# Three partial products of one tile: two PSUM banks joined on VectorE, or one bank scaled in place by ScalarE

## The chip, the cores and the metric

The kernel runs on one core of one Trainium2 chip. The metric is the device time of that core in microseconds, from the first instruction to the last. The five engines of the core are written PE (TensorE: matmuls; PEld are its weight loads), DVE (VectorE), ACT (ScalarE), POOL (GpSimd) and SP (the queue that starts most transfers).

## The reference, cut to what matters

The input is 64 batches of 256 rows by 512 columns. Two layers follow one another, each of the form "add to x, then normalise each row".

```python
q = x @ Wq + bq;  k = x @ Wk + bk;  v = x @ Wv + bv        # 8 heads of 64
scores = q @ k^T / 8, masked by adj                         # per batch and head, 256 x 256
attn = softmax(scores);  out = (attn @ v) @ Wo + bo
x = layernorm(x + out)                                      # layer 0
y = adj @ x                                                 # per batch
x = layernorm(x + y @ weight + bias)                        # layer 1
```

All arrays are float32. The change concerns only the three products q, k and v.

## The kernel before, in words

**Pairs and windows.** The 64 batches are worked in 32 pairs, two batches at a time, so that a product with 128 columns of weights and a pair's 512 rows is one PSUM tile of 128 x 512 float32 (a bank). The program is unrolled: one "window" for each pair. A window holds the four attention units of its own pair (`scores` at L391, the exponentials at L395, `values` at L418 and L426), and between them the products q, k, v of the next pair and the rest of the pair before: the projection with Wo (`o_proj`), the product with adj (`adj_x`, L541) and layer 1's product (`last`).

**Who decides the order.** TensorE's order is written out by hand: the function `between(w)` returns the list of steps of one window, in which an entry `None` (a "slot") stands for the `values` of one unit and the `scores` of the next. The other engines' orders come from a scheduler that puts instructions by its own estimate of when they are ready. Each engine then works through its list in that order. Small steps that VectorE does later are put off by a count of steps (`later`, `tick`).

**The products q, k, v.** In this profile a 128x512 matmul on whole float32 operands (L343) lasts 592 to 649 ns in the mean, and one on parts of the type fp32r (L350) 389 to 423 ns. From the third pair on each operand is therefore split in parts: x into `high`, `low` and `diff` (`XG`, `XL`, `XD` in the code; `x_parts`, L176 to L178, and `x_high`, L321), and each weight likewise, once, into three parts that lie in DRAM and are streamed back in a ring of five buffers named `wr` (`load_w`, L141, issued by GpSimd). A tile of q, k or v is the sum of three products of parts; `FINE` is 4096:

```python
tile = (1 + 1/FINE) * (high @ w_high + low @ w_low) + diff @ w_diff
```

Each product is a group of four matmuls (L350). `part_products` puts the first two into one bank, called near, and the third into another, called far. `joined` brings them together: ScalarE evicts near to SBUF with the scale (and the bias of q or k) at L355, and VectorE adds far to that at L357. There are 12 such tiles in a window (four each of v, q and k); q and k tiles go to `qT` and `kT`, v tiles to `v`. The first two pairs have no parts: there each tile is one product on the whole float32 operands (L343).

**Other products.** `o_proj` and `last` use a scheme of seven block products instead of eight (`SEVEN`, `block_product`, L281), each of eight matmuls, whose results VectorE adds to the rows `r` (L331, L502). The sums of blocks that they need are made by VectorE at L241. After the last block VectorE takes the statistics (L467, L468), adds epsilon (`ve`, L473), GpSimd takes the power -1/2 (`rstd`, L475), and the rows are normalised: in layer 0 by VectorE (L489), in layer 1 by ScalarE (L487, after `less` at L477). For `adj_x` the normalised rows are split once more, `hl` and `ys`, the high part by ScalarE (L526), the low one by VectorE (L527).

**Attention.** Exponentials from PSUM by ScalarE (L395), mask by VectorE (L400), sum of the two key halves (L406); the row sums and the weighted values are evicted by ScalarE to `zc` (L420) and `vc` (L429); VectorE turns the sums around (`z`, L436; reciprocal, L439; `zc`, L441) and divides (`o`, L442). The biases are added to the rows at L458. The next pair's x is transposed by VectorE (L311).

**PSUM.** There are two pools of four banks each: `ps_at` (tiles named `at`) for attention, `ps_mm` (tiles named `mm`) for all else.

Of a middle window, `between` gave this order before (v, q, k are whole tiles; o, y, l are `o_proj`, `adj_x`, `last`):

```python
seq = slot + v[:2] + o[:1] + v[2:3] + o[1:2] + v[3:] + o[2:3] + slot + o[3:4] + q[:1] + o[4:5] + q[1:2] + \
    o[5:] + q[2:] + slot + y[:2] + k[:1] + y[2:] + k[1:2] + bo_steps[:1] + l[:1] + k[2:3] + bo_steps[1:] + \
    l[1:2] + k[3:] + after_k
```

It is followed by a slot and the other five blocks of `last`, mixed with the transposes and splits of the pair after next.

Of the kernel before, what the change touches and what calls it, by code (L numbers as in the profile page):

```python
# [20 lines left out]
F32 = mybir.dt.float32  # L21
F32R = mybir.dt.float32r
I32 = mybir.dt.int32
AF = mybir.ActivationFunctionType
OP = mybir.AluOpType
AX = mybir.AxisListType

P = 128
# [3 lines left out]
FINE = 4096.0  # L32
# [5 lines left out]
def tile_adj_resnorm(tc, x, adj, wq, bq, wk, bk, wv, bv, wo, bo, w1, b1, out):  # L38
    good = fast(tc, x, adj, wq, bq, wk, bk, wv, bv, wo, bo, w1, b1, out)
    with tc.If(good < P):  # L40
        general(tc, x, adj, wq, bq, wk, bk, wv, bv, wo, bo, w1, b1, out)


def fast(tc, x, adj, wq, bq, wk, bk, wv, bv, wo, bo, w1, b1, out):

    nc = tc.nc
    B, N, D = x.shape
    HD = D // H
    DC = D // P
    NC = N // P  # L50
    NP = B // 2
# [21 lines left out]
    four = pool("four", 4)  # L73
    small = pool("small", 2)
    ps_at = pool("ps_at", 4, space=bass.MemoryType.PSUM)
    ps_mm = pool("ps_mm", 4, space=bass.MemoryType.PSUM)

    XC, R, XF, XG, XL, XD, Q, K, V, E, SM, O, HL, Y, ST = ({} for _ in range(15))
# [23 lines left out]
    def weights(name, w, b12, queue, by_head=False):  # L102

        t = W[name] = cpool.tile([P, 7, 2, HF], F32, name="w" + name)
        b12 = B12[name] = one.tile([P, 2, 2, HF], F32, name=b12)[:, 0]
        for to, k, n in ((t[:, 0], 0, 0), (t[:, 1], 1, 0), (b12, 0, 1), (t[:, 2], 1, 1)):
            quarter = w[k * HF:(k + 1) * HF, n * HF:(n + 1) * HF]
            if by_head:  # L110
                for a in range(2):
                    queue.dma_start(to[:, a], quarter.rearrange("(h a i) e -> a h i e", h=4, a=2)[a])
            else:
                queue.dma_start(to, quarter.rearrange("(c p) e -> p c e", p=P))
# [9 lines left out]
    def by_partition(b, name):  # L124
        t = cpool.tile([P, DC], F32, name=name)
        nc.sync.dma_start(t, b.rearrange("(c p) -> p c", p=P))
        return t
# [7 lines left out]
    WP, SCRATCH = {}, {}  # L135
# [8 lines left out]
    FIRST = {}  # L144
# [40 lines left out]
    bq_s, bk_s = by_partition(bq, "bq"), by_partition(bk, "bk")  # L185
# [83 lines left out]
    BANKS = {}  # L269
# [63 lines left out]

    def part_products(name, p, j, rows_first):


        near = ps_mm.tile([P, D], F32, name="mm")
        if p < 2:  # L340
            for k in range(DC):
                left, right = (XF[p, k], FIRST[name, k]) if rows_first else (FIRST[name, k], XF[p, k])
                nc.tensor.matmul(near, left[:, j * P:(j + 1) * P], right, start=k == 0, stop=k == DC - 1)  # L343
            return near, None
        far = ps_mm.tile([P, D], F32, name="mm")
        for i, (xs, to) in enumerate(((XG, near), (XL, near), (XD, far))):
            for k in range(DC):
                a, b = xs[p, k], WP[name, p, i](k)
                left, right = (a, b) if rows_first else (b, a)
                nc.tensor.matmul(to, left[:, j * P:(j + 1) * P], right, start=k == 0 and i != 1,  # L350
                                 stop=k == DC - 1 and i != 0)
        return near, far

    def joined(to, near, far, **kw):
        nc.scalar.activation(to, near, AF.Identity, scale=1 + 1 / FINE if far else 1.0, **kw)  # L355
        if far:
            nc.vector.tensor_tensor(to, to, far, op=OP.add)  # L357

    def q_or_k(p, j, is_k):
        T, b, name = (K, bk_s, "k") if is_k else (Q, bq_s, "q")  # L360
        g, a = divmod(j, 2)
        if a == 0:
            T[p, g] = qk.tile([P, 2, 2, N], F32, name=name + "T")
        joined(T[p, g][:, a].rearrange("p b i -> p (b i)"), *part_products(name, p, j, False), bias=b[:, j:j + 1])

    def v_rows(p, j):
        b, c = divmod(j, 2)
        if c == 0:
            V[p, b] = four.tile([P, NC, D], F32, name="v")
        joined(V[p, b][:, c], *part_products("v", p, j, True))  # L370

    def q_cols(p, j):
        q_or_k(p, j, False)

    def k_cols(p, j):
        q_or_k(p, j, True)

# [244 lines left out]
    def between(w):  # L624

        pre = [w + 1] if w + 1 < NP else []
        post = [w - 1] if w >= 1 else []
        a = lambda f, n: [(f, p, i) for p in pre for i in range(n)]
        z = lambda f, n: [(f, p, i) for p in post for i in range(n)]
        o, l, y = z(o_proj, 7), z(last, 7), z(adj_x, 4)  # L630
        v, q, k = a(v_rows, 4), a(q_cols, 4), a(k_cols, 4)
        bo_steps = [(with_bo, w, b) for b in range(2) if 0 <= w < NP]
        x_steps = [(x_t, w + 2, i) for i in range(4) if w + 2 < NP]
        x_parts_ = [(x_parts, w + 2, i) for i in range(4) if w + 2 < NP]
        x_all = [s for pair in zip(x_steps, x_parts_) for s in pair]
        load = lambda *what: [(load_w, n, w + 1 + d, i) for n, d, i in what]
        slot = [None]
        if w == -1:
            seq = [(x_t, 0, i) for i in range(4)]
            split_v, split_q = ([(split_w, n, i) for i in range(4)] for n in "vq")  # L640
            for i in range(4):
                seq += v[i:i + 1] + split_v[i:i + 1]
            for i in range(4):
                seq += q[i:i + 1] + split_q[i:i + 1]
            seq += [(adj_t,)]
            for i in range(4):
                seq += k[i:i + 1] + x_steps[i:i + 1]
            return seq + load(("v", 2, 0), ("v", 2, 1), ("v", 2, 2), ("q", 2, 0), ("q", 2, 1))
        if w == 0:
            weights("1", w1, "hl", nc.sync)  # L650
            split_k = [(split_w, "k", i) for i in range(4)]
            return slot + v + [(weight_sums, "1"), (weights, "o", wo, "hl", nc.sync, True)] + slot + q[:3] + split_k + \
                slot + q[3:] + k[:1] + [(bv_wo,), (weight_sums, "o"), (load_r, 0)] + k[1:2] + slot + k[2:] + bo_steps + \
                x_all + [(load_r, 1)]
        v += load(("q", 0, 2), ("k", 0, 0), ("k", 0, 1))
        q += load(("k", 0, 2), ("v", 1, 0), ("v", 1, 1))
        after_k = load(("v", 1, 2), ("q", 1, 0), ("q", 1, 1)) if w + 2 < NP else []
        seq = slot + v[:2] + o[:1] + v[2:3] + o[1:2] + v[3:] + o[2:3] + slot + o[3:4] + q[:1] + o[4:5] + q[1:2] + \
            o[5:] + q[2:] + slot + y[:2] + k[:1] + y[2:] + k[1:2] + bo_steps[:1] + l[:1] + k[2:3] + bo_steps[1:] + \
            l[1:2] + k[3:] + after_k  # L660
        if w < NP - 2:
            return seq + slot + [s for i in range(5) for s in l[2 + i:3 + i] + x_all[2 * i:2 * i + 2]]
        o0 = [(part, w, 0, 0, i) for i in range(7)]
        return seq + l[2:3] + slot + l[3:4] + o0[:1] + l[4:5] + o0[1:3] + l[5:6] + o0[3:5] + l[6:] + o0[5:]

    def window(w):
        units = [(w - 1, 3)] + [(w, u) for u in range(4)]
        for step in between(w):
            if step is None:
                before = units.pop(0)  # L670
                if before[0] >= 0:
                    values(*before)
                scores(*units[0])
            else:
                f, *args = step
                f(*args)
            tick()
# [195 lines left out]
```

## Time and profile before

| what | value |
| --- | --- |
| time, median of 3 runs | 2662.22 us (2661.95 to 2664.72) |
| span of the profiled run | 2662.8 us |
| PE busy | 2588.0 us, 97% |
| DVE busy | 2108.1 us, 79% |
| ACT busy | 962.5 us, 36% |
| POOL busy | 288.0 us, 11% |
| additions at L357, q, k and v, 120 each | 82.3, 82.2 and 82.1 us of DVE |
| evictions at L355, q, k and v, 128 each | 87.4, 88.2 and 72.8 us of ACT |

Busy times are sums over the span. Matmuls are pipelined, and the ends that the profile gives them are modelled, so a PE that is busy need not be at its peak; starts of matmuls are what one can measure distances with. Busy time of an engine says nothing about whether the end waits for that engine: for this one reads the chain of waits, which is followed back from the last instruction, at each step to what released it.

### The profile page before, as it was taken

Reading aid. Unit: us, or ns where it says so; the run is one execution under the profiler, and the core shown is the slowest. Engines: PE = TensorE matmul, PEld = TensorE weight load, DVE = VectorE, ACT = ScalarE, POOL = GpSimd, SP = SyncE. Lnnn points to the kernel's source line nnn. Section 1 sums busy time; section 2 is a strip of 40 time slices with the busy share of each in tenths; the row PEclk is TensorE's granted clock in tenths of the full one; section 3 lists DMA queues with packets and bytes.
Section 4 is the critical chain, followed back from the end, with each engine's and each line's share of the span. In section 5 each row is a group of like instructions: output and inputs, shape, how many; then the busy total and the mean of one; then the engine's idle time right before and its main releaser. Section 6 shows DMA issues by size and latency. Waiting matters only on the chain.

```text
span 2662.8 us, 41800 instructions
## 1 busy us (share of the span) xinstructions
PE 2588.0 (97%) x16326; PEld 1990.5 (75%) x16326; DVE 2108.1 (79%) x3561; ACT 962.5 (36%) x1710; POOL 288.0 (11%) x610
## 2 busy tenths in 40 slices
PE   9999999999999999999999999999999999999997
PEld 4577777777777777777777777777777777777775
DVE  3777878878788778788787888787887788887877
ACT  4433333333333333333333333333333333333333
POOL 0011101111101111011111011110111110111000
PEclk9999999999999999999999999999999999999999
DMA  9444655544564536554545555365545455454310
GB/s 274 133 150 136 184 149 150 151 164 153 144 189 134 164 132 188 143 162 140 174 143 154 179 143 159 137 180 143 173 139 169 138 165 168 143 159 149 121 37 29
DMA packets 346987, 402.04 MB, mean 151 GB/s; under 512 B 270240, under 2 KB 272544, under 8 KB 312224
## 3 DMA queue, kind: packets, MB, share of 16 engines
q0 software_dynamic: 38880, 283.13, 29.0%
q1 hardware_dynamic: 307360, 115.13, 20.3%
q8 instruction: 130, 2.13, 0.3%
q10 hardware_dynamic: 544, 1.05, 0.1%
q14 instruction: 73, 0.60, 0.1%
HBM read 356.26 MB, written 42.99 MB: 150 GB/s over the span
## 4 chain that ended last, share of the span: by engine, by line
PE 68%; DVE 21%; ACT 5%; issue 4%; POOL 1%; DMA 1%; DVEq 0%; SPq 0%; POOLq 0%; ACTq 0%
PE mm L350 30%; PE mm L281 19%; PE mm L541 5%; PE at L391 5%; PE at L426 4%; DVE e L400 3%; DVE xT L311 3%; DVE st L467 3%; ACT r L487 3%; PE mm L343 2%; DVE diff L178 2%; DVE low L177 2%; DVE sm L406 1%; DVE r L331 1%; PE at L418 1%
## 5 line engine op out<-in xcount | busy, mean ns | idle before, releaser
L400 DVE TENSOR_TENSOR e<-e,adjT 128x1024 f32<-128x1024 f32 x256 | 307.1, 1221 | 27.7 <-ACT e L395 27.7
L350 PE MATMUL mm<-high,wr 128*128 128x512 f32 x960 | 288.0, 421 | 0.0
L395 ACT ACTIVATE e<-at 128x512 f32<-128x512 f32 x512 | 269.4, 596 | 49.1 <-PE at L391 49.0
L391 PE MATMUL at<-qT,kT 64*128 64x256 f32 x2048 | 264.0, 393 | 7.7 <-ACT zc L420 4.0
L281 PE MATMUL mm<-wo,o 128*128 128x256 f32 x1024 | 249.1, 385 | 15.9 <-ACT v L355 15.9
L350 PE MATMUL mm<-low,wr 128*128 128x512 f32 x960 | 257.9, 390 | 0.0
L350 PE MATMUL mm<-diff,wr 128*128 128x512 f32 x960 | 256.7, 389 | 0.0
L391 PEld LDWEIGHTS at<-qT,kT 64*128 64x128 f32 x2048 | 197.0, 187 | 75.8 <-issue 53.0
L426 PE MATMUL at<-e,v 128*32 128x256 f32 x4096 | 244.5, 379 | 0.0
L281 PEld LDWEIGHTS mm<-wo,o 128*128 128x128 f32 x1024 | 189.2, 189 | 63.6 <-ACT v L355 28.1
L281 PE MATMUL mm<-w,o 128*128 128x256 f32 x992 | 235.9, 380 | 0.0
L331 DVE TENSOR_TENSOR r<-r,mm 128x512 f32<-128x512 f32 (+1 forms) x204 | 132.3, 650 | 120.9 <-PE mm L281 120.8
L355 ACT ACTIVATE qT<-mm,bq 128x512 f32<-128x512 f32 x128 | 87.4, 683 | 364.7 <-PE mm L350 353.6
L350 PEld LDWEIGHTS mm<-low,wr 128*128 128x128 f32 x960 | 180.3, 188 | 40.2
L281 PEld LDWEIGHTS mm<-w,o 128*128 128x128 f32 x992 | 186.0, 190 | 30.4 <-issue 0.3
L350 PEld LDWEIGHTS mm<-diff,wr 128*128 128x128 f32 x960 | 180.2, 188 | 37.9
L281 PE MATMUL mm<-w,ys 128*128 128x256 f32 x720 | 179.1, 392 | 26.3 <-DVE r L502 26.3
L350 PEld LDWEIGHTS mm<-high,wr 128*128 128x128 f32 x960 | 176.7, 188 | 30.1
L426 PEld LDWEIGHTS at<-e,v 128*32 128x32 f32 x4096 | 133.1, 110 | 87.9
L321 ACT ACTIVATE high<-x 128x512 fp32r<-128x512 f32 x120 | 75.7, 630 | 305.7 <-DVE x L176 235.3
L281 PEld LDWEIGHTS mm<-w,ys 128*128 128x128 f32 x720 | 129.6, 189 | 71.2 <-DVE r L502 37.9
L502 DVE TENSOR_TENSOR r<-r,mm 128x512 f32<-128x512 f32 x240 | 162.1, 675 | 21.9 <-PE mm L281 21.9
(141 smaller groups left out, 4106.9 us busy)
## 6 DMA issues: line engine op xcount, KB each, us to landing
wr<-v POOLq DMA_DIRECT2D x90, 1024.0 KB, 8.0
wr<-q POOLq DMA_DIRECT2D x90, 1024.0 KB, 7.9
wr<-k POOLq DMA_DIRECT2D x90, 1024.0 KB, 6.9
r<-in_x_dram SPq DMA_DIRECT2D x32, 1024.0 KB
x<-in_x_dram SPq DMA_DIRECT2D x496, 64.0 KB
out_dram<-r SPq DMA_DIRECT2D x60, 512.0 KB
out_dram<-r SPq DMA_DIRECT2D x8, 256.0 KB
o<-in_L_gnn_Wv_dram ACTq DMA_DIRECT2D x2, 512.0 KB
```

Of the source, the lines that this page charges most:

```text
L281: nc.tensor.matmul(pm[:, j, :], left[:, k, j * P:(j + 1) * P], right[:, k, :], start=begins and j == 0 and k == 0, stop=k == 1, skip_group ...
L311: nc.vector.transpose(XF[p, i], xs)
L331: nc.vector.tensor_tensor(to, to, pm, op=OP.add)
L350: nc.tensor.matmul(to, left[:, j * P:(j + 1) * P], right, start=k == 0 and i != 1, stop=k == DC - 1 and i != 0)
L355: nc.scalar.activation(to, near, AF.Identity, scale=1 + 1 / FINE if far else 1.0, **kw)
L391: nc.tensor.matmul(sc[s][:, a, :], K[p, g][r, a, b, kc * P:(kc + 1) * P], Q[p, g][r, a, b, :], start=True, stop=True)
L395: nc.scalar.activation(e[:, s], sc[s], AF.Exp, scale=qscale)
L400: nc.vector.tensor_tensor(e, e, mask[:, kc:kc + 1, :].to_broadcast([P, 4, N]), op=OP.mult)
L426: nc.tensor.matmul(at[h * 32:(h + 1) * 32, a, :], V[p, b][:, kc, col:col + 32], e[kc][:, h % 2, h // 2, :], start=kc == 0, stop=kc == NC - 1)
L467: nc.vector.bn_stats(st, R[p][:, b, c, :])
L502: assembled(i, pm, out, lambda to, pm, half: nc.vector.tensor_tensor(to, to, pm, op=OP.add))
L541: nc.tensor.matmul(pm[:, j, :], hl[:, i, mc, j * P:(j + 1) * P], adjT[:, mc, :], start=mc == 0 and i == 0, stop=mc == NC - 1 and i == 1)
```

## The change

All three products go into one bank. `near` makes the first two, and ScalarE then multiplies the bank in place by 1 + 1/4096 (PSUM to PSUM). `far` has TensorE add the third product to the scaled contents (its first matmul doesn't set the flag that begins a new sum), and ScalarE evicts the finished tile, with the bias for q and k. VectorE's addition of far is gone. A tile so needs one bank where it needed two, but its three products can't follow one another directly: the third waits for the scaling. The written order therefore puts other work between a tile's near and its far.

```diff
-    def part_products(name, p, j, rows_first):
...
-        far = ps_mm.tile([P, D], F32, name="mm")
-        for i, (xs, to) in enumerate(((XG, near), (XL, near), (XD, far))):
...
-    def joined(to, near, far, **kw):
-        nc.scalar.activation(to, near, AF.Identity, scale=1 + 1 / FINE if far else 1.0, **kw)
-        if far:
-            nc.vector.tensor_tensor(to, to, far, op=OP.add)
+    def near(name, p, j):
...
+        pm = BANKS[name, p, j] = ps_mm.tile([P, D], F32, name="mm")
...
+        for i, xs in enumerate((XG, XL)):
+            part_product(pm, name, p, j, i, xs)
+        nc.scalar.activation(pm, pm, AF.Copy, scale=1 + 1 / FINE)
+    def part_product(pm, name, p, j, i, xs):
+        for k in range(DC):
+            nc.tensor.matmul(pm, *operands(name, j, xs[p, k], WP[name, p, i](k)), start=i == 0 and k == 0,
+                             stop=k == DC - 1, skip_group_check=True)
+    def far(name, p, j):
+        pm = BANKS.pop((name, p, j))
+        if p > 1:
+            part_product(pm, name, p, j, 2, XD)
+        if name == "v":
...
+            nc.scalar.activation(V[p, b][:, c], pm, AF.Copy)
+            return
...
+        nc.scalar.activation(T[p, g][:, a].rearrange("p b i -> p (b i)"), pm, AF.Identity, bias=bias[:, j:j + 1])
```

The order of a middle window becomes this, with vn, qn, kn for the near and vf, qf, kf for the far steps. The loads of weight parts (not shown) are moved along with the steps that last read a buffer.

```diff
-        seq = slot + v[:2] + o[:1] + v[2:3] + o[1:2] + v[3:] + o[2:3] + slot + o[3:4] + q[:1] + o[4:5] + q[1:2] + \
-            o[5:] + q[2:] + slot + y[:2] + k[:1] + y[2:] + k[1:2] + bo_steps[:1] + l[:1] + k[2:3] + bo_steps[1:] + \
-            l[1:2] + k[3:] + after_k
+        seq = slot + vn[:2] + vf[:1] + o[:1] + vf[1:2] + vn[2:3] + o[1:2] + vf[2:3] + vn[3:] + o[2:3] + vf[3:] + slot + \
+            o[3:4] + qn[:1] + o[4:5] + qf[:1] + qn[1:2] + o[5:6] + qf[1:2] + qn[2:3] + o[6:] + qn[3:] + qf[2:3] + slot + \
+            qf[3:] + y[:2] + kn[:1] + y[2:] + kf[:1] + kn[1:2] + bo_steps[:1] + kn[2:3] + kf[1:2] + l[:1] + kf[2:3] + \
+            kn[3:] + bo_steps[1:] + l[1:2] + kf[3:]
```

In the text below, L numbers are those of the kernel before unless it says otherwise.

More of the change, by code (lines that the diff above doesn't have):

```diff
@@ L331, in assembled @@
             nc.vector.tensor_tensor(to, to, pm, op=OP.add)
-    def part_products(name, p, j, rows_first):
-        near = ps_mm.tile([P, D], F32, name="mm")
+    def near(name, p, j):
+        pm = BANKS[name, p, j] = ps_mm.tile([P, D], F32, name="mm")
         if p < 2:
[L341 to L344, printed above, removed]
-        far = ps_mm.tile([P, D], F32, name="mm")
-        for i, (xs, to) in enumerate(((XG, near), (XL, near), (XD, far))):
[L347 to L352, printed above, removed]
@@ L354, in joined @@
-    def joined(to, near, far, **kw):
-        nc.scalar.activation(to, near, AF.Identity, scale=1 + 1 / FINE if far else 1.0, **kw)
-        if far:
-            nc.vector.tensor_tensor(to, to, far, op=OP.add)
-    def q_or_k(p, j, is_k):
-        T, b, name = (K, bk_s, "k") if is_k else (Q, bq_s, "q")
+            whole_product(pm, name, p, j)
+            return
+        for i, xs in enumerate((XG, XL)):
+            part_product(pm, name, p, j, i, xs)
+        nc.scalar.activation(pm, pm, AF.Copy, scale=1 + 1 / FINE)
@@ new lines, in operands, with whole_product @@
+    def operands(name, j, rows, w):
+        left, right = (rows, w) if name == "v" else (w, rows)
+        return left[:, j * P:(j + 1) * P], right
+    def whole_product(pm, name, p, j):
+        for k in range(DC):
+            nc.tensor.matmul(pm, *operands(name, j, XF[p, k], FIRST[name, k]), start=k == 0, stop=k == DC - 1)
+    def part_product(pm, name, p, j, i, xs):
+        for k in range(DC):
+            nc.tensor.matmul(pm, *operands(name, j, xs[p, k], WP[name, p, i](k)), start=i == 0 and k == 0,
+                             stop=k == DC - 1, skip_group_check=True)
@@ L361, in q_or_k @@
+    def far(name, p, j):
[3 more added lines that the diff above has]
+        if name == "v":
+            b, c = divmod(j, 2)
+            if c == 0:
+                V[p, b] = four.tile([P, NC, D], F32, name="v")
+            nc.scalar.activation(V[p, b][:, c], pm, AF.Copy)
+            return
+        T, bias = (K, bk_s) if name == "k" else (Q, bq_s)
         g, a = divmod(j, 2)
@@ L363, in q_or_k @@
             T[p, g] = qk.tile([P, 2, 2, N], F32, name=name + "T")
[L364 to L376, printed above, removed]
+        nc.scalar.activation(T[p, g][:, a].rearrange("p b i -> p (b i)"), pm, AF.Identity, bias=bias[:, j:j + 1])
     UNITS = [(g, b) for g in range(2) for b in range(2)]
@@ L627, in between @@
         post = [w - 1] if w >= 1 else []
-        a = lambda f, n: [(f, p, i) for p in pre for i in range(n)]
         z = lambda f, n: [(f, p, i) for p in post for i in range(n)]
         o, l, y = z(o_proj, 7), z(last, 7), z(adj_x, 4)
-        v, q, k = a(v_rows, 4), a(q_cols, 4), a(k_cols, 4)
+        first, then = ([[(f, n, p, j) for j in range(4) for p in pre] for n in "vqk"] for f in (near, far))
         bo_steps = [(with_bo, w, b) for b in range(2) if 0 <= w < NP]
@@ L637, in between @@
         slot = [None]
+        if w < 1:
+            v, q, k = ([s for pair in zip(m, n) for s in pair] for m, n in zip(first, then))
         if w == -1:
@@ L641, in between @@
             for i in range(4):
-                seq += v[i:i + 1] + split_v[i:i + 1]
+                seq += v[2 * i:2 * i + 2] + split_v[i:i + 1]
             for i in range(4):
-                seq += q[i:i + 1] + split_q[i:i + 1]
+                seq += q[2 * i:2 * i + 2] + split_q[i:i + 1]
             seq += [(adj_t,)]
             for i in range(4):
-                seq += k[i:i + 1] + x_steps[i:i + 1]
+                seq += k[2 * i:2 * i + 2] + x_steps[i:i + 1]
             return seq + load(("v", 2, 0), ("v", 2, 1), ("v", 2, 2), ("q", 2, 0), ("q", 2, 1))
@@ L651, in between @@
             split_k = [(split_w, "k", i) for i in range(4)]
-            return slot + v + [(weight_sums, "1"), (weights, "o", wo, "hl", nc.sync, True)] + slot + q[:3] + split_k + \
-                slot + q[3:] + k[:1] + [(bv_wo,), (weight_sums, "o"), (load_r, 0)] + k[1:2] + slot + k[2:] + bo_steps + \
+            return slot + v + [(weight_sums, "1"), (weights, "o", wo, "hl", nc.sync, True)] + slot + q[:6] + split_k + \
+                slot + q[6:] + k[:2] + [(bv_wo,), (weight_sums, "o"), (load_r, 0)] + k[2:4] + slot + k[4:] + bo_steps + \
                 x_all + [(load_r, 1)]
-        v += load(("q", 0, 2), ("k", 0, 0), ("k", 0, 1))
-        q += load(("k", 0, 2), ("v", 1, 0), ("v", 1, 1))
-        after_k = load(("v", 1, 2), ("q", 1, 0), ("q", 1, 1)) if w + 2 < NP else []
-        seq = slot + v[:2] + o[:1] + v[2:3] + o[1:2] + v[3:] + o[2:3] + slot + o[3:4] + q[:1] + o[4:5] + q[1:2] + \
-            o[5:] + q[2:] + slot + y[:2] + k[:1] + y[2:] + k[1:2] + bo_steps[:1] + l[:1] + k[2:3] + bo_steps[1:] + \
-            l[1:2] + k[3:] + after_k
+        (vn, qn, kn), (vf, qf, kf) = first, then
+        vn += load(("q", 0, 2), ("k", 0, 0))
+        vf += load(("k", 0, 1))
+        qn += load(("k", 0, 2), ("v", 1, 0))
+        qf += load(("v", 1, 1))
+        kn += load(("v", 1, 2), ("q", 1, 0))
+        kf += load(("q", 1, 1))
+        seq = slot + vn[:2] + vf[:1] + o[:1] + vf[1:2] + vn[2:3] + o[1:2] + vf[2:3] + vn[3:] + o[2:3] + vf[3:] + slot + \
+            o[3:4] + qn[:1] + o[4:5] + qf[:1] + qn[1:2] + o[5:6] + qf[1:2] + qn[2:3] + o[6:] + qn[3:] + qf[2:3] + slot + \
+            qf[3:] + y[:2] + kn[:1] + y[2:] + kf[:1] + kn[1:2] + bo_steps[:1] + kn[2:3] + kf[1:2] + l[:1] + kf[2:3] + \
+            kn[3:] + bo_steps[1:] + l[1:2] + kf[3:]
         if w < NP - 2:
```

## The prediction

> **What bounds the kernel now.** I read the page's busy row first, then its chain of waits, then that chain in order of time over one window, then VectorE's timeline in one stretch.
>
> ```profile
> PE 2588.0 (97%) x16326; PEld 1990.5 (75%) x16326; DVE 2108.1 (79%) x3561; ACT 962.5 (36%) x1710; POOL 288.0 (11%) x610
> ...
> PE 68%; DVE 21%; ACT 5%; issue 4%; POOL 1%; DMA 1%; DVEq 0%; SPq 0%; POOLq 0%; ACTq 0%
> ```
>
> TensorE looks full, and yet the chain spends 32% of the span elsewhere. So one part of each window is TensorE's, and in another TensorE runs beside a longer chain of others. The chain in order of time shows where they meet; the columns are start, length, what.
>
> ```profile
> 1018.53 0.17 DVE less L477
> ...
> 1019.45 2.21 ACT r L487 x3
> 1021.66 0.96 ACT e L395 x2
> 1022.62 0.49 ACT v L355
> ...
> 1023.15 1.99 PE mm L281 x8
> ...
> 1047.47 3.45 PE mm L281 x16
> 1050.93 5.46 PE mm L350 x24
> 1056.39 0.57 PE at L418 x8
> ...
> 1060.62 2.08 PE mm L541 x16
> 1062.70 2.73 PE mm L350 x12
> 1065.43 2.15 PE mm L541 x16
> ...
> 1076.53 2.08 PE mm L350 x9
> 1078.61 0.02 issue
> 1078.64 0.69 DVE diff L178
> ...
> 1102.84 0.96 ACT e L395 x2
> 1103.80 0.49 ACT v L355
> ```
>
> The same eviction of v ends at 1023.11 and at 1104.29: a window is 81.18 us. From 1023.15 to 1078.61 the chain is TensorE alone (the table by stage has it busy 55.45 of 55.45 us). From 1078.64 to 1104.3, 25.7 us, it is VectorE (x's transposes and splits, masks, sums, statistics), GpSimd's power, ScalarE's four normalisations at L487, two exponentials, and the eviction of the first v tile. TensorE's matmuls in that second stretch lie in the shadow and cost nothing. This is a loop: a window is TensorE's own stretch plus the VectorE/ScalarE stretch. Work that TensorE takes out of the shadow lengthens it.
>
> A second chain is nearly as long as TensorE's work, from the last o_proj block (ends 1050.93) to the y matmuls that read `hl` (1065.43):
>
> ```profile
> 1051.24 0.66 DVE L502 TENSOR_TENSOR r<-r,mm 128x512 f32<-128x512 f32 x1
> ...
> 1057.83 0.68 DVE L357 TENSOR_TENSOR qT<-qT,mm 128x512 f32<-128x512 f32 x1
> ...
> 1064.81 0.68 DVE L527 TENSOR_TENSOR hl<-r,hl 128x512 fp32r<-128x512 f32 x1
> ```
>
> The low half of `hl` is done at 65.49 while TensorE reaches those matmuls at 65.43. VectorE's chain is 65.49 - 50.93 = 14.56 us, TensorE's work beside it 14.50: no slack. The waits agree: "PEld mm L541 <- DVE hl L527" already totals 11.8 us.
>
> [...] L355 waited behind L487 and L395 above with its data long there. [...] after TensorE's 4.01 us gap before 109.30 the table by stage has a granted clock of 0.73 from 110 to 120.
>
> **The change part by part.** The same matmuls run. A group of four 128x512 matmuls takes 2.73 / 3 = 0.91 us; a tile of q, k or v is three groups.
>
> Removed: 12 additions at L357 per window (q, k, v), 0.685 us each, 8.2 us of VectorE. Most lie in TensorE's stretch, where VectorE is busy 41.09 of 55.45 us: worth nothing there. Two matter: the last kT addition, in the first chain, and one qT addition (1057.83) in the second. The other late qT addition ran while VectorE awaited GpSimd's power.
>
> Added: 12 in-place scalings on ScalarE per window. No row shows PSUM to PSUM; the nearest is v's eviction without a bias pointer, 592 ns [...]. I take 0.6; 0.5 (two in a row start 0.5 apart: the two exponentials take 1.05) and 0.7 (with a bias pointer, 0.687) bound it. The evictions stay. That is 7 us more in 81 on an engine 36% busy: throughput is no matter. What matters is the new wait: "far" waits for the scaling, and TensorE's order puts everything after far behind it. In the built lists most fars come at least one other block or near (1.7 to 1.8 us) after their own near, longer than 0.2 + 0.6. Behind far in TensorE's queue stands everything else; o_proj's evictions and so VectorE wait for that in turn. Two places fail.
>
> **A, start of v.** TensorE's new order is near0, near1, far0, then o_proj's first block. ScalarE's new list still has the second exponentials, L487 four times and two more exponentials ahead of the scalings, as before. So the scaling of near0 ends when the eviction of v's first tile ended, and TensorE resumes at the same point of the first chain. But until then it had six groups to do, and now has four. In the window shown TensorE's timeline has the six groups' starts from 1016.85 to 1021.56; the sixth is issued by 1022.47, and the restart came at 1023.15: an idle of 0.7 us. Now it idles from the end of the fourth, at 1020.65: 2.5 us. Two groups leave the shadow, that is +1.82. Against it, at the start of the first chain (k's last group, at 1078.21) the kT addition falls away, but the eviction L331 of the `last` block that now stands just ahead comes in. With the delays of other blocks (L331 starts 0.39 after the group that follows its block and takes 0.68, then diff 0.6 to the next start) the next transpose starts at +1.60 instead of +1.78. A = 1.82 - 0.18 = 1.64 us.
>
> **B, between o_proj and y.** Near of q's third tile now stands ahead of the last o_proj block (two groups), and far of k's first tile behind the y matmuls (one). TensorE's work between falls by 3 x 0.91 = 2.73, from 14.50 to 11.77 us. VectorE's chain from the block's end E: r starts at E+0.04 (not +0.31, since the statistics of the block ahead are done by then), and by the old spacing of 3.52 the power ends at +3.56. But VectorE's new list has z and its reciprocal ahead of L489's four, and z waits for zc of the next slot: L418 starts at about E+2.7, and in the neighbouring slot the reciprocal ended 1.8 after it (1034.05 to 1035.85). So L489 starts at +4.5, `hl` 1.83 later at +6.35, `ys` 0.6 later, and then by the old start-to-start steps: 0.61 to zc, 0.36 to L458, 1.10 to o, 0.60 to the masks, 2.39 to the sum, 1.15 to `hl`, 0.68 long: E+13.84. TensorE, there at +11.77, waits 2.1 us, of which it waits about 0.1 already: B = 2.0 us. On ScalarE `vc` now comes behind `hl` and `ys`, so that the scores wait for its bank some 1.4 us; that lies inside the 2.0, because the second chain ends later than the scores do.
>
> PSUM: one bank per tile instead of two, held longer; going through the list I find no block that waits for one beyond these. The weight loads move with their last readers; the tightest, q's third part, is issued after near of v's last tile, some 12 us of TensorE work ahead of its use, against 8 us to landing. Startup (two pairs without parts) keeps its work, and the tail has no q, k, v: nothing.
>
> Sum: A in 29 windows (the wait of L281 for L355 occurs 29 times) 47.6; B in 30 windows 60. 2662.2 + 107.6 = 2770 us.
>
> **The rivals.** R1, only A holds: VectorE's second chain shortens more than I think. For: 8.2 us less on VectorE; against: that stretch loses a single addition of 14.56 us. 2662 + 48 = 2710. R2, faster: VectorE's relief moves the first chain forward and the two recurring waits (26.3 for L502, 15.9 for L355, plus weight loads, about 50 in all) vanish. For: VectorE is busy 24.60 of 25.70 us there; against: only one of the 12 additions lies in it, and the list shows no reordering of L487. 2662 - 50 = 2612. R3, [...] the clock halves: the halving after 109.30 lasted some 6.7 us (mean clock 0.89 over 104 to 110 and 0.73 over 110 to 120: 2 x (0.11 x 6 + 0.27 x 10)) and so lost about 3.4; 2770 + 29 x 3.4 = 2869. [...] against: the gap that did it was 4.0 us.
>
> **How the numbers follow.** Forecast 0.74; R1 or between it and the forecast 0.12; R2 0.06; R3 0.06; no change has 0.02 of these, where both gains and losses would have to cancel. The range: A between 1.3 and 1.9, B between 1.2 and 2.7 with the scaling's bounds gives 2736 to 2798; I widen to 2725 and 2805 for half of R1's region and small waits on ScalarE's queue. Faster 0.06, same 0.02, slower 0.92.
>
> **What would show it.** A: TensorE's first far of v waits for the scaling some 2.5 us, 29 times. B: the waits of the scores (for vc) and of the y matmuls (for `hl`) come to some 2 us in each of 30 windows. VectorE's busy time falls by 360 x 0.685 = 247 us, ScalarE's rises by about 360 x 0.6 = 216, and a window is 81.2 + 3.6 = 84.8 us long. Wrong if the normalisations end earlier against near0, or if VectorE's second chain is under 12 us.

## The result and the profile after

| | before | after |
| --- | --- | --- |
| time, median | 2662.8 us | 2787.9 us |
| ratio | | 1.047 (1.045 to 1.049) |
| span of the profiled run | 2662.8 us | 2786.2 us |
| length of a middle window | 81.17 us | 84.70 us in 15 windows, 86.1 to 86.3 in 13 |

The lengths are distances between the same slot's first matmul in successive windows, over 28 windows. In this part line numbers of the changed kernel and of its variants are those of their own listings: L345 is the scaling in place, L357 the products of parts, L368 and L374 the evictions, and L389, L393, L418, L427, L485, L500, L525 and L539 are before's L391, L395, L420, L429, L487, L502, L527 and L541.

The page's busy row and the engines' shares of the chain:

```profile
PE 2623.4 (94%) x16326; PEld 2007.2 (72%) x16326; DVE 1884.7 (68%) x3201; ACT 1167.2 (42%) x2070; POOL 296.9 (11%) x610
...
PE 55%; DVE 22%; DMA 10%; ACT 6%; issue 5%; POOL 1%; SPq 1%; DVEq 0%; POOLq 0%; ACTq 0%
```

VectorE lost 223 us of busy time and ScalarE gained 205, somewhat less than the 247 and 216 that were forecast at full length for each operation. TensorE's share of the chain fell from 68% to 55%: it no longer carries the stretch of the window that was its own. The DMA's 10% is a load of x at which the view enters VectorE's run at the sum of masks; VectorE is not idle ahead of that sum, so I don't read it as a wait.

The waits of TensorE (time in all, how often, longest), in the kernel before and then in the changed one:

```profile
PE mm L281 <- DVE r L502: 26.3, 29, 0.9
PE mm L281 <- ACT v L355: 15.9, 29, 0.7
...
PE at L391 <- ACT vc L429: 3.7, 1, 3.7
...
PE mm L541 <- DVE hl L527: 1.9, 3, 0.9
```

```profile
PE mm L357 <- ACT mm L345: 68.9, 29, 2.5
...
PE mm L281 <- DVE r L500: 25.9, 29, 0.9
PE at L389 <- ACT vc L427: 22.2, 31, 3.6
PE mm L539 <- DVE hl L525: 18.7, 33, 0.9
```

Of the changed kernel's, the second is as before. The first, third and fourth are new or grown; the old wait of L281 for v's bank is gone. The new ones stand in the chain in order of time as follows; the last two lines are of the next window.

```profile
1064.16 2.21 ACT r L485 x3
1066.37 0.96 ACT e L393 x2
1067.33 0.49 ACT mm L345
...
1067.86 2.07 PE mm L357 x4
1069.94 2.31 PE mm L281 x8
...
1099.02 1.73 PE mm L281 x8
1100.75 2.75 PE mm L357 x12
1103.50 0.02 issue
1103.52 0.69 ACT qT L374
1104.21 0.30 ACT zc L418
...
1105.29 1.79 DVE r L487 x4
...
1113.79 0.69 DVE hl L525
...
1114.53 2.04 PE mm L539 x15
...
1154.01 1.19 PE mm L357 x4
1155.21 1.73 PE mm L281 x8
```

At 1067.33 the scaling of v's first tile ends the same run of normalisations and exponentials that the eviction ended before. From 1103.52 to 1114.5 VectorE and ScalarE now lead up to the y matmuls, where TensorE had led. The third thing is in the two pairs of PE lines. The same four matmuls last 2.07 us at 1067.86 and 1.19 at 1154.01, the eight after them 2.31 and 1.73. The table by stage, over 3.4 us before and after each of these two restarts, says why; its columns are the stretch, its length, busy time (and number of instructions) of PE, PEld, DVE, ACT and POOL, then granted clock, DMA share and GB/s:

```profile
1064.40:1067.80 3.40, 1.07 (x5) 0.56 (x3) 3.37 (x5) 3.40 (x7) 0.00 (x0) 0.97 0.56 206
1067.90:1071.30 3.40, 3.40 (x9) 2.72 (x10) 2.47 (x3) 0.99 (x2) 0.00 (x0) 0.55 0.47 120
1150.50:1153.90 3.40, 1.12 (x5) 0.58 (x4) 3.37 (x5) 3.40 (x7) 0.00 (x0) 1.00 0.54 199
1154.00:1157.40 3.40, 3.39 (x15) 2.92 (x16) 2.95 (x4) 1.04 (x2) 0.00 (x0) 1.00 0.48 124
```

After one idle the clock is 0.55, after another of the same length it is 1.00. The record of the granted clock goes to 0.50 for 3.41 us after 13 of these idles, and the 13 long windows are those.

### The profile page after: what moved, and what is told of

Its sections match the earlier page's. It is cut to its first block, busy times and chain, and to the rows that moved or that the text cites. A ratio compares the mean times of both kernels' runs of the same rounds, so it can differ in the third digit from the quotient of the medians.

```text
span 2786.2 us, 41470 instructions
## 1 busy us (share of the span) xinstructions
PE 2623.4 (94%) x16326; PEld 2007.2 (72%) x16326; DVE 1884.7 (68%) x3201; ACT 1167.2 (42%) x2070; POOL 296.9 (11%) x610
## 4 chain that ended last, share of the span: by engine, by line
PE 55%; DVE 22%; DMA 10%; ACT 6%; issue 5%; POOL 1%; SPq 1%; DVEq 0%; POOLq 0%; ACTq 0%
PE mm L357 28%; PE mm L281 17%; DMA x<-in_x_dram 10%; DVE e L398 3%; PE mm L539 3%; DVE st L465 3%; PE at L389 2%; ACT r L485 2%; PE mm L353 2%; PE at L424 2%; DVE r L487 2%; DVE xT L311 2%; DVE low L177 2%; DVE diff L178 1%; DVE hl L525 1%
## 5 line engine op out<-in xcount | busy, mean ns | idle before, releaser
L345 ACT ACTIVATE mm<-mm 128x512 f32<-128x512 f32 x360 | 206.5, 579 | 428.4 <-PE mm L357 428.4
L500 DVE TENSOR_TENSOR r<-r,mm 128x512 f32<-128x512 f32 x240 | 163.5, 681 | 268.6 <-PE mm L281 268.6
L389 PE MATMUL at<-qT,kT 64*128 64x256 f32 x2048 | 279.5, 394 | 26.2 <-ACT vc L427 22.2
L393 ACT ACTIVATE e<-at 128x512 f32<-128x512 f32 x512 | 268.7, 596 | 40.1 <-PE at L389 40.1
L357 PE MATMUL mm<-diff,wr 128*128 128x512 f32 x960 | 284.8, 418 | 0.0
L389 PEld LDWEIGHTS at<-qT,kT 64*128 64x128 f32 x2048 | 199.1, 186 | 107.7 <-issue 53.0
L357 PE MATMUL mm<-high,wr 128*128 128x512 f32 x960 | 269.7, 403 | 0.0
L357 PE MATMUL mm<-low,wr 128*128 128x512 f32 x960 | 256.7, 389 | 0.0
L281 PE MATMUL mm<-wo,o 128*128 128x256 f32 x1024 | 256.2, 393 | 0.0
L281 PE MATMUL mm<-w,o 128*128 128x256 f32 x992 | 235.8, 380 | 0.0
L281 PEld LDWEIGHTS mm<-wo,o 128*128 128x128 f32 x1024 | 200.2, 198 | 41.9 <-issue 9.9
L357 PE MATMUL mm<-wr,diff 128*128 128x512 f32 x480 | 160.7, 459 | 68.9 <-ACT mm L345 68.9
L281 PEld LDWEIGHTS mm<-w,o 128*128 128x128 f32 x992 | 186.0, 190 | 30.4 <-issue 0.3
L357 PEld LDWEIGHTS mm<-low,wr 128*128 128x128 f32 x960 | 180.2, 188 | 38.0
L357 PEld LDWEIGHTS mm<-diff,wr 128*128 128x128 f32 x960 | 176.3, 188 | 40.5 <-issue 9.9
L357 PEld LDWEIGHTS mm<-high,wr 128*128 128x128 f32 x960 | 178.4, 188 | 35.7
L281 PE MATMUL mm<-w,ys 128*128 128x256 f32 x720 | 179.2, 392 | 25.9 <-DVE r L500 25.9
L281 PEld LDWEIGHTS mm<-w,ys 128*128 128x128 f32 x720 | 129.6, 189 | 70.8 <-DVE r L500 37.5
```

What stands on the lines that cost most here:

```text
L281: nc.tensor.matmul(pm[:, j, :], left[:, k, j * P:(j + 1) * P], right[:, k, :], start=begins and j == 0 and k == 0, stop=k == 1, skip_group ...
L345: nc.scalar.activation(pm, pm, AF.Copy, scale=1 + 1 / FINE)
L357: nc.tensor.matmul(pm, *operands(name, j, xs[p, k], WP[name, p, i](k)), start=i == 0 and k == 0, stop=k == DC - 1, skip_group_check=True)
L389: nc.tensor.matmul(sc[s][:, a, :], K[p, g][r, a, b, kc * P:(kc + 1) * P], Q[p, g][r, a, b, :], start=True, stop=True)
L393: nc.scalar.activation(e[:, s], sc[s], AF.Exp, scale=qscale)
L500: assembled(i, pm, out, lambda to, pm, half: nc.vector.tensor_tensor(to, to, pm, op=OP.add))
```

## The experiments

My theory: the loss has three parts, A (v's first far waits behind ScalarE's normalisations), B (VectorE's chain to `hl` outlasts TensorE's work), and the halved clock that A's idle brings on. Rivals: the near-to-far round trip costs something at each of 12 tiles; ScalarE's load; the two places give gains back to one another. Edits are against the changed kernel unless said otherwise.

**A alone undone** (`e1`): o_proj's first block and near of v's third tile stand ahead of v's first and second far.

```diff
-        seq = slot + vn[:2] + vf[:1] + o[:1] + vf[1:2] + vn[2:3] + o[1:2] + ...
+        seq = slot + vn[:2] + o[:1] + vn[2:3] + vf[:2] + o[1:2] + ...
```

> The changed kernel with only the start of v reordered: near0, near1, o_proj's first block, near2, and only then far0, far1. My theory (term A: near0's scaling stands behind the normalisations on ScalarE, and TensorE has too little to do until then): 3.8 + 1.7 + 1.8 = 7.3 us of matmuls stand where the scaling is ready after 6.35, so the 2.5 us idle goes, and with it the halved clocks: 2788 - 29 x 2.5 - 22 = about 2693 us, each window 82.2 us. Rival (every near-to-far round trip costs a little, the sum over 12 tiles is the loss): only one tile's wait changes, 2775 or more.

Measured: 2692.6 us, ratio to before 1.011 (1.009 to 1.013), windows of 82.05 to 82.2 us throughout. The wait for L345 is gone from TensorE's waits, and so are the halved clocks in the middle windows (the mean granted clock is 0.995, against the changed kernel's 0.988); the other waits stand as they did (22.2 and 18.6 us). The rival of a cost at every tile falls: all twelve scalings are still there, and TensorE waits for none of them.

**B alone undone** (`e2`): the last o_proj block ahead of near of q's third tile.

```diff
-... qf[1:2] + qn[2:3] + o[6:] + qn[3:] + qf[2:3] + slot + \
+... qf[1:2] + o[6:] + qn[2:] + qf[2:3] + slot + \
```

> The changed kernel with only the last o_proj block moved ahead of near of q's third tile, so that TensorE has 1.82 us more to do between it and the y matmuls. My theory (term B: VectorE's chain from that block to hl is longer than TensorE's work beside it): the waits of the scores for vc and of the y matmuls for hl, together about 1.9 us in 30 windows, go: 2788 - 56 = about 2732 us, while the idle before far0 stays at 2.5 us. Rival (those waits come from ScalarE's fuller queue and stay): about 2788 us.

Measured: 2755.5 us, ratio 1.035 (1.033 to 1.036): 23 us short of the gain I expected. TensorE's waits in this kernel:

```profile
PE mm L357 <- ACT mm L345: 69.2, 29, 2.7
...
PE mm L539 <- DVE hl L525: 9.3, 33, 0.9
...
PE at L389 <- ACT vc L427: 3.7, 1, 3.7
```

The scores' wait is gone (the 3.7 left are one wait in the start), the y matmuls' is halved. Nine windows take 83.1 to 83.5 us, 1.6 less than 84.70, and nineteen some 84.8. So B's mechanism holds. Some of its wait remains (0.3 us a window by the line above, 0.44 by `e7` below), and the rest of the shortfall is the clock: it is halved in 19 of the 28 windows instead of 13 (a mean of 0.983).

**Both** (`e3`).

> Both reorderings at once. My theory: A and B are separate places and add up: 2693 - 56 = about 2637 us, 80.3 us a window, about 1 % faster than before, because with neither wait the kernel keeps the first chain's relief and loses the old 0.7 us wait for a bank too. Rival (one place's gain is given back at the other, since both feed one loop): no better than the better of the two alone, about 2693 us.

Measured: 2646.0 us, ratio 0.994 (0.992 to 0.995), 80.50 us a window. 84.70 - 2.63 (A's edit) - 1.57 (B's edit) = 80.50: they add up, and the rival of gains given back falls. The 9 us over the expectation are B's edit again, which gives 1.57 us a window and not the 1.9 expected; a wait for `hl` is left, 9.4 us in this kernel's list.

**The clock by itself** (`e4`): matmuls that nothing reads fill A's idle.

```diff
+    def filler(p):
+        pm = ps_mm.tile([P, D], F32, name="mm")
+        for i, xs in enumerate((XG, XL)):
+            part_product(pm, "v", p, 1, i, xs)
...
-        seq = slot + vn[:2] + vf[:1] + o[:1] + ...
+        seq = slot + vn[:2] + [(filler, p) for p in pre] + vf[:1] + o[:1] + ...
```

> The changed kernel with eight more matmuls (the second near of v once more, into a bank that nothing reads) in the 2.5 us in which TensorE waits for near0's scaling. The wait's end stays, so only the clock can change. My theory (14 of 29 windows are 1.6 us longer because the clock is halved for 3.4 us after the idle): every window takes 84.7 us, 2788 - 14 x 1.6 = about 2766 us. Rival (the longer windows come from transfers or from the profile's own variation): 2788 us or, with 29 x 1.8 us more work, up to 2840.

Measured: 2769.1 us, 1.8 us of matmuls more in each window and 19 us faster than the changed kernel. TensorE's timeline at the place (near of the second tile, the filler, far, o_proj; its L362 is the products):

```profile
1056.18 1.07 PE L362 MATMUL mm<-wr,high 128*128 128x512 f32 x4
1057.09 1.07 PE L362 MATMUL mm<-wr,low 128*128 128x512 f32 x4
1057.99 1.07 PE L362 MATMUL mm<-wr,high 128*128 128x512 f32 x4
1058.90 1.07 PE L362 MATMUL mm<-wr,low 128*128 128x512 f32 x4
1060.54 1.21 PE L362 MATMUL mm<-wr,diff 128*128 128x512 f32 x4 [0.57 <-ACT mm L345]
1061.59 1.89 PE L281 MATMUL mm<-wo,o 128*128 128x256 f32 x8
```

Far still waits for the scaling, but behind 0.57 us of idle instead of 2.4, every middle window takes 84.6 to 84.8 us, and none of them has a halved clock (a mean of 0.995). That settles the long windows.

**VectorE's relief alone** (`e5`), an edit of the kernel before: the additions for q and k left out, so that q and k lack their third product.

```diff
-        if far:
+        if far and not kw:
             nc.vector.tensor_tensor(to, to, far, op=OP.add)
```

> The kernel before with VectorE's additions for q and k left out (240 of 360; the third product of q and k is computed but not added, so q and k lack a part), v as it was, the order as it was. It measures what VectorE's relief alone is worth. My theory: only the last kT addition lies in the chain from k's last group to v's eviction, whose next transpose would start at +1.05 instead of +1.78 us: 29 x 0.7 = 20 us, about 2643 us. Rival (VectorE binds, at 79 % busy, and each addition counts): 8 x 0.685 us in 30 windows are 164 us, about 2500; half of it, 2580.

Measured: 2653.0 us, ratio 0.995 (0.994 to 0.997), 80.80 us a window. Eight additions of 0.685 us, 5.5 us of VectorE, give 0.37 us of 81.17. The rival of VectorE as the bound falls. I expected 0.7 from the first chain alone. Its places in order of time:

```profile
1014.67 0.17 DVE less L477
...
1019.30 1.99 PE mm L281 x8
...
1074.53 0.70 DVE diff L178
```

TensorE's stretch, from the restart at L281 to `diff`, takes 55.23 us, against 55.49 before (1078.64 less 1023.15): the weight loads of the y matmuls waited 11.8 us in all for `hl` before and 2.4 here. From `less` to `diff` it is 59.86 us, so from `diff` to the next `less` 80.80 - 59.86 = 20.94, against 21.06 before (1099.70 less 1078.64). So the missing addition shortened the first chain by 0.12 us only. The transpose behind `diff` does start at once (1075.26), but half of the 0.6 us won there is taken up by a step `x` (L176) that stands ahead of `ve` in this kernel's list for VectorE (1093.71) and behind `less` in before's (1099.78); the rest I can't place.

**The scaling doubled** (`e6`): two scalings in place for all tiles but v's first.

```diff
-        nc.scalar.activation(pm, pm, AF.Copy, scale=1 + 1 / FINE)
+        if (name, j) == ("v", 0):
+            nc.scalar.activation(pm, pm, AF.Copy, scale=1 + 1 / FINE)
+        else:
+            for _ in range(2):
+                nc.scalar.activation(pm, pm, AF.Copy, scale=math.sqrt(1 + 1 / FINE))
```

> The changed kernel with the in-place scaling of 11 of 12 tiles in two steps (each by the square root of the factor), the first v tile's left as it is: ScalarE gets 330 x 0.58 = 191 us more. My theory (the scaling is hidden everywhere but at v's first tile): 2788 to 2796 us, the few us where q's scalings stand ahead of zc. Rival (ScalarE's load or the near-to-far round trip is what costs): 0.58 us more at each far, up to 2788 + 190 = 2978 us.

Measured: 2786.0 us against the changed kernel's 2787.9. ScalarE's busy time rises by 186 us to 1352.8 and the time hardly moves. Nearly all windows without a halved clock take 84.75 to 84.8 us, up to 0.1 more than the changed kernel's. The clock is halved in 11 windows instead of 13 (a mean of 0.989), which hides that in the total. ScalarE's load and the round trip at eleven of the twelve tiles cost next to nothing: the spacing in the written order covers them.

**More work beside the chain to hl** (`e7`), on top of both reorderings: near of k's second tile ahead of the last two y blocks.

```diff
-... y[:2] + kn[:1] + y[2:] + kf[:1] + kn[1:2] + bo_steps[:1] + kn[2:3] + ...
+... y[:2] + kn[:2] + y[2:] + kf[:1] + bo_steps[:1] + kn[2:3] + ...
```

> As the kernel with both reorderings, and near of k's second tile also ahead of the last two y blocks, 1.82 us more beside VectorE's chain to hl. My theory: the rest of that wait (9.4 us in all by the waits) goes, 80.2 us a window, about 2637 us. Rival (the wait is for ScalarE's high part or for a bank, not for VectorE's low part): 2646 us as it is, or more where the y blocks now wait for a bank.

Measured: 2630.0 us, ratio to before 0.987 (0.985 to 0.988), windows of 80.0 to 80.1 us but for one of 80.4. That is 16 us less than with both edits, where 9 were expected: the line for `hl` had shown only part of that wait, since TensorE's weight loads waited 19.4 us for it with both edits and 2.4 here. What is left of the two waits, and the one that recurs:

```profile
PE mm L281 <- DVE r L500: 25.9, 29, 0.9
...
PE mm L539 <- DVE hl L525: 1.7, 3, 0.9
```

This is the fastest version of all that ran, with the changed kernel's arithmetic and three changes of order.

**The additions put back** (`e8`), on top of that: after each eviction of a tile made of parts VectorE takes the maximum of the tile with itself, an operation of the old addition's size (680 to 686 ns in the mean, the additions 684 to 686) that leaves the values as they are.

```diff
-        nc.scalar.activation(T[p, g][:, a].rearrange("p b i -> p (b i)"), pm, AF.Identity, bias=bias[:, j:j + 1])
+        to = T[p, g][:, a].rearrange("p b i -> p (b i)")
+        nc.scalar.activation(to, pm, AF.Identity, bias=bias[:, j:j + 1])
+        if p > 1:
+            nc.vector.tensor_tensor(to, to, to, op=OP.max)
```

(and the same after the eviction of v)

> As the kernel with both reorderings and k, with a VectorE operation of 128x512 (the maximum of the finished tile with itself) put back for each of 360 tiles in the place of the old addition. If the gain over the kernel before comes from the bank that each tile no longer needs, and so from the freedom of order, and not from VectorE's relief: 2637 to 2645 us, still faster than before. Rival (the relief of VectorE gives the gain): at 0.7 us in each window or more, back to 2660 us or above.

Measured: 2634.6 us, ratio 0.989 (0.987 to 0.990), windows of 80.18 us. Its busy row:

```profile
PE 2579.7 (98%) x16326; PEld 2001.5 (76%) x16326; DVE 2097.8 (80%) x3561; ACT 1161.4 (44%) x2070; POOL 288.9 (11%) x610
```

VectorE is nearly as loaded as before the change (2108.1), ScalarE carries the scalings on top, and the kernel is still 1.1% faster than before; putting 360 operations back cost 4.7 us. So most of what the change has to give doesn't come from VectorE's relief. It comes from the order: by the starts of matmuls TensorE's idle in a window is shorter than before by 0.69 us at v's bank (a wait that is gone), 0.18 at L502's `r` and 0.12 at `hl`, together the 0.99 between 81.17 and 80.18. That this order needs the one bank per tile is argued, not tried: it has three near tiles and an o_proj block begun ahead of the first far, four banks of the pool's four, where two banks begun together for each tile, as the kernel before has them, would make seven. Another order for the kernel before, with two banks, was not tried either, so it stays open how much of the gain it could have had.

## Why the prediction was right

**A loop of two stretches, with TensorE's work in the second one free.** Right. The predicted window was 84.8 us, and the windows without a halved clock take 84.70.

**A = 1.64 us, 2.5 us idle 29 times.** Right in the main: 29 waits, idle by the starts of matmuls of 2.5 us in nearly all, against 0.69 before. That is 1.84 more, where 1.82 was forecast for the two groups. The 0.18 set against it came to 0.06: the transpose starts 1.72 us after k's last group (1043.43 after 1041.71), not 1.60. By its own steps A is so 1.78; as what B leaves of the longer window it is 84.70 - 81.17 - 1.9 = 1.6, and the 0.15 us between the two stay open. Undoing A gave 2.63, because that order removes the whole idle, with the 0.69 that before had as the wait for v's bank.

**B = 2.0 us.** Right, both in cause and size: the two edits that put work back beside VectorE's chain took 1.57 and 0.44 us (80.50 to 80.06) off the window, 2.0 in all. About 0.1 of that was a wait that before had too (by the starts of matmuls its y stretch is 0.12 longer than `e7`'s), which leaves 1.9. The steps came as reckoned: in the chain above, from the end of the last o_proj block at 1100.75, L487 starts at +4.54 (4.5 was forecast) and the low half of `hl` ends at +13.73 (13.84). The waits stood where they were put: scores for vc, y matmuls for `hl`.

**Everything else at nothing.** Right to 0.1 us: ScalarE's extra load (e6), the other eleven waits for a scaling (e1, e6), banks and weight loads (no such wait in TensorE's list). The price of a scaling was 579 ns in the mean, against the 0.6 us taken.

**VectorE's relief worth little.** Right in kind: by e5, 0.37 us of a window for 8 additions. That an earlier transpose moves the end of the first chain by as much is not so: in e5 it started 0.6 us earlier and the chain ended 0.12 earlier.

**R3, the halved clock, was given 6 chances in 100 and taken as all or nothing, at 3.4 us in each of 29 windows.** That is the step that failed, and it is the 18 us between forecast and result. The argument was that the one gap seen to do it lasted 4.01 us; that 2.5 would not do was an estimate that no trace showed. The runs show that a gap of 2.5 does it in 13 of 29 windows. They lose 1.5 us each (86.2 less 84.70), 13 x 1.5 = 20 us, and e4, which fills the idle, gave 19 us back and lies 1 us from the forecast. All-or-nothing fails too: of the 27 idles of 2.50 to 2.56 us, 12 were followed by half the clock and 15 were not, so the length of a gap alone did not decide it.

## What to carry to other kernels

Where a chain of waits shows TensorE alone in one stretch and other engines alone in another, matmuls in the second stretch are free, and moving them out of it costs their full length however small the wait that moved them; count the work that stands beside a chain, not only the new wait. A tile that is finished in two steps with another engine between them wants the first step early and the second late, and the first such tile behind a busy queue needs the most work in between. A bank or buffer that a change frees may be worth more than the operations it saves, but only once the order uses it (here that the order needs the bank was argued, not tried).

## What the runs showed of the hardware

- In the changed kernel 13 of the 29 idles before far, which last 2.47 to 2.71 us (from the last start ahead plus 0.23, the usual distance, to the next start), were followed by a granted clock of 0.50 for 3.41 us each, 16 were not. The 13 halvings begin at whole multiples of 3.413 us from one another (299.58 less 214.25 is 85.33, 25 times that), and the window of 84.70 us is no such multiple (24.8 times). That an idle's place in time decides, and not its length alone, is an estimate from these numbers that no run tested by itself. After the 4.01 us gap of the kernel before, the clock was 0.50 for 6.83 us.
- In e2, with windows of 83.13 us where the clock was whole, 20 of the 29 idles were followed by half the clock, at 1.67 us each (84.80 less 83.13), which makes 33 us instead of 20. The mean granted clock was 0.983, against 0.988.
- 128x512 scaled from PSUM to PSUM by ScalarE takes 579 ns in the mean, evicted to SBUF without a bias pointer 592 (before's v tiles) and 598 (the changed kernel's).
